# Eight dense chunks an image in every group, six indirect transfers under way, and shorter planned times for them

## The chip, the cores and the metric

The program runs on one core of a Trainium2 chip. The metric is the device time of one execution in microseconds. Five engines work side by side, each through its own queue in order: TensorE (PE in the profile, its weight loads PEld), VectorE (DVE), ScalarE (ACT), GpSimd (POOL) and SyncE (SP). Here SP issues the plain DMAs, and POOL issues only indirect ones (scatters and gathers of rows by a list of row numbers).

## The reference

The input is 32 images of 128 channels by 56 x 56 pixels, f32. Cut to what matters:

```python
x = x + conv3x3(sign(group_norm(x)), sign(w)) * Alpha      # 128 -> 128 channels
t = to_tokens(x)                                            # 3136 tokens of 128 numbers an image
n = layer_norm(t)
t = t + (n @ Wq) * sum_over_tokens((n @ Wk) * (n @ Wv))
n = layer_norm(t)
p = softmax(n @ router_w); top_p, top_i = top_k(p, 2)       # 8 experts, two of them a token
top_p = top_p / sum(top_p)
t = t + sum_k top_p[k] * (n @ expert_w[top_i[k]])           # and expert_b
out = from_tokens(t)
```

So every token goes through two of eight 128 x 128 expert matrices, and its result is put back where it came from.

## The kernel before

An image's 3136 tokens are cut into 25 chunks of 128 (the last has 64); four chunks make a block. The first stages (convolution, statistics, the token product, the projection, the router) run for every image alike. The experts are done in one of two ways.

**Dense.** The first `DENSE[group]` chunks of an image take all eight experts and weight them by gates that are zero for the six not chosen. For a block, `spread` (line 1087, its broadcast 1096, on SP) loads the gates of two experts at a time, broadcast over 128 partitions (`bc`, 512 KB); `gated` (1105, DVE) multiplies the tokens by them; `experts` (1117 and 1123, PE) sums the products in one bank; `finish` (1134, DVE) adds; `store` (1139) writes out. A block is four such units of two experts, after one turn of its tokens to channels (1078 PE, 1085 ACT).

**Sorted.** The remaining chunks of an image are sorted by pair of experts. `pair_of`, `places` and `row_numbers` (lines 1200 to 1280) give each token a row in a list of its group; `row_add` (1319, ACT) finishes a chunk's rows, and `scatter` (1325, POOL) writes its 128 rows to the list in DRAM with one indirect DMA. When all images of a group are scattered, its tiles are worked through in quads of four: `tile_load` (1617, SP), `tile_turn` (1624, PE), `tile_turned` (1630, ACT), `tile_experts` (1642, PE: just the two experts of the tile), `tile_read` (1660 and 1667, ACT), `tile_sum` and `tile_out` (1672, 1677, DVE), `tile_store` (1685, SP). When all tiles of a group are stored, `gather` (1400, POOL) brings the results of each chunk back with one indirect DMA; `back_turn` (1415, PE), `back_out` (1423, ACT) and `back_store` (1427, SP) write a block of four chunks out.

The 28 first images form groups of 8, 8, 8 and 4. The last four images belong to no group and are wholly dense, so that they lie beside the last group's tiles and gathers. Three places tie POOL to the other engines: an image's token buffer (three of them, tile `tok`) is free for the next image only when all its scatters have landed; a group's first tile load waits for all its scatters; a group's first gather waits for all its tile stores, and each gather needs one of 14 buffers that `back_turn` empties.

**What sets the order.** Nothing is issued in the order of the loops. Each step is entered with `at(due, key, engine, work, ...)`: a due time, an engine, a planned duration, the steps it follows, the rings of buffers that it takes and frees, and `delay`, the planned time until its result has landed. `in_order` (line 108) plays these steps through on a clock of its own, always taking, of the steps that can start first, the most urgent one, and so writes down one order for all engines. PE, DVE and ACT then run in exactly that order; POOL's and SP's instructions stand in it too. The durations there are constants in the source and not times of the chip; a wrong one changes only the order. A POOL step, scatter or gather, is planned at 2.0, a gather lands 12.0 after it, and in the plan POOL takes one step at a time.

`in_turn` (line 1475) adds a real wait: each indirect transfer waits until the one `IN_FLIGHT` places before it has landed, so that at most four are under way.

Of the kernel before, what the change touches and what calls it, by code (L numbers as in the profile page):

```python
# [66 lines left out]
ROW = C + 4  # L67
N_PAIR = N_EXP * (N_EXP - 1) // 2
GROUPS = (8, 8, 8, 4)
DENSE = (8, 8, 12, 12)  # L70

IN_ORDER = {mybir.EngineType.PE, mybir.EngineType.DVE, mybir.EngineType.Activation}
NEWTON = 3
IN_FLIGHT = 4

GATE_LANDS, SPREAD_LANDS, STORE_LANDS, TILE_LANDS, GATHER_LANDS = 5.0, 6.5, 5.0, 6.0, 12.0
TILE_PACE = (0.7, 0.6, 0.4, 0.3)
GATHER_PACE = (1.0, 0.8, 0.5, 0.4)
N_Q = C + 2 * N_EXP
# [98 lines left out]
def conv_attn_moe_kernel(  # L178
# [35 lines left out]

    most = n_ck - min(DENSE)
    group_of, last_of = {}, []
    for g, n in enumerate(GROUPS):
        for _ in range(n):
            group_of[len(group_of)] = g
        last_of.append(len(group_of) - 1)  # L220
    group_rows = [n * (n_tok - k * C) for n, k in zip(GROUPS, DENSE)]
    region = max(group_rows) + C
# [230 lines left out]
    def at(due, key, engine, work, do, *args, after=(), take=(), free=(), delay=0.0, slack=0.0):  # L453


        if isinstance(work, float):
            steps[key] = Step(due, key, engine, work, do, args, after, take, free, delay, slack, 0.0)
            return
        running = []

        def go_on():
            if not running:
                running.append(do(*args))
            next(running[0], None)

        lag = LAG if isinstance(work, list) else 0.0
        for j, w in enumerate(work):
            last = j == len(work) - 1
            part = key if last else (*key, "part", j)
            steps[part] = Step(  # L470
                due, part, engine, w, go_on, (), [(*key, "part", j - 1)] if j else after,
                [] if j else take, free if last else [], delay if last else 0.0, slack, lag,
            )

    def base(i):

        n = len(group_of)
        return P * (min(i, n) + 1.2 * max(0, i - n))
# [39 lines left out]
    def last_dense(i):  # L518
        return DENSE[group_of[i]] // PER - 1 if i in group_of else n_blk - 1

    def plan_image(i: int):
        s = base(i)
        d = {}
        st1, st2, lgp = st1_all[i % 2], st2_all[i % 2], lgp_all[i % 2]
        move = move_all[i % 2]
        n_dense = DENSE[group_of[i]] if i in group_of else n_ck
        n_sort = n_ck - n_dense
# [135 lines left out]
        for g in range(n_blk):  # L663
            b = min(n_conv - 1, (cols_of(g)[1] - 1) // (ROWS * width))
            due = s + 4 + 5.5 * b
# [689 lines left out]
        for k, c in enumerate(range(n_dense, n_ck)):  # L1355
            at(
                s + 138 + 2 * k, ("row_add", i, c), "ACT", 0.30, row_add, c,
                after=[("row_scalars", i), ("row_numbers", i), ("project_add", i, c // Q_GROUP)],
                take=["sent"],
            )  # L1360
            at(
                s + 140 + 2 * k, ("scatter", i, c), "POOL", 2.0, scatter, c,
                after=[("row_add", i, c), ("row_numbers", i), ("open", group)],
                free=[("tok", ("xt", i, 0)), ("sent", ("row_add", i, c))], delay=3.0,
            )
# [65 lines left out]
        begin, each = gather_due(group)  # L1431
        due = begin + each * (i - last_of[group] + GROUPS[group] - 1)
# [5 lines left out]
        k = 0  # L1438
        for b in range(n_dense // PER, n_blk):
            share = len(blocks[b]) / PER  # L1440
            for c in blocks[b]:
                at(
                    due + each * k / n_sort, ("gather", i, c), "POOL", 2.0, gather, c,
                    after=[("result_rows", i)]
                    + [("gather", i, c - 1) if k else ("gather", i - 1, n_ck - 1)]
                    + [("tile_store", group, q) for q in range(quads_of(group))],
                    take=["back"], delay=GATHER_LANDS,
                )
                k += 1
            at(  # L1450
                due + each * k / n_sort + 5, ("back_turn", i, b), "PE", 0.45 * share, back_turn, b,
                after=[("gather", i, c) for c in blocks[b]], take=["ps"],
                free=[("back", ("gather", i, c)) for c in blocks[b]],
            )
            at(
                due + each * k / n_sort + 6, ("back_out", i, b), "ACT", 0.47 * share, back_out, b,
                after=[("back_turn", i, b)], take=["o"], free=[("ps", ("back_turn", i, b))],
            )
            at(
                due + each * k / n_sort + 8, ("back_store", i, b), "SP", 0.35, back_store, b,  # L1460
                after=[("back_out", i, b)], free=[("o", ("back_out", i, b))], delay=STORE_LANDS,
            )
# [12 lines left out]
    def in_turn(dma):  # L1475

        before = moved[-IN_FLIGHT:][:1] if len(moved) >= IN_FLIGHT else []
        for b in before:
# [10 lines left out]
    def quads_of(g):  # L1489
        return -(-tiles_of(g) // PER)  # L1490
# [5 lines left out]
    def gather_due(g):  # L1496

        begin, each = tiles_due(g)
        return begin + each * quads_of(g) + 15, GATHER_PACE[g] * P
# [187 lines left out]
    def plan_group(g):  # L1687
# [29 lines left out]
        for q in range(quads_of(g)):  # L1717
# [4 lines left out]
                + [("tile_load", g, q - 1) if q else ("tile_load", g - 1, quads_of(g - 1) - 1)]  # L1722
                + [("scatter", i, c) for i in members for c in range(DENSE[g], n_ck)],
                take=["t_in"], delay=TILE_LANDS,
# [37 lines left out]
    for i in range(n_img):  # L1762
        plan_image(i)
# [57 lines left out]
```

## Time and profile before

| what | value |
|---|---|
| median of 14 runs | 2242.15 us (2235.4 to 2251.95) |
| profiled execution, its own time | 2251.51 us |
| span from first to last instruction | 2249.7 us |
| PE busy | 2093.0 us, 93% of the span |
| DVE busy | 1977.2 us, 88% |
| ACT busy | 1526.3 us, 68% |
| POOL busy | 1009.5 us, 45%, nearly all in 428 scatters and 428 gathers |
| granted TensorE clock, mean | 0.973 |
| DMA moved | 448.56 MB |

The profile is of one execution, which took 9.4 us more than the median. Busy time is the time in which an engine had at least one instruction under way. A row of the groups gives line, engine, operation, tiles written and read, shapes and count, then busy time and the mean duration of one instruction (they overlap on PE, so that count times mean is more than busy), then the idle time just before them and what ended it. An f32 matrix product stands as two instructions. The chain is followed back from the last instruction, at each step to whatever released it; its shares say in which work the end was waited for.

### The profile page before, as it was taken

Reading aid. Unit: us, or ns where it says so; the run is one execution under the profiler, and the core shown is the slowest. Engines: PE = TensorE matmul, PEld = TensorE weight load, DVE = VectorE, ACT = ScalarE, POOL = GpSimd, SP = SyncE. Lnnn points to the kernel's source line nnn. Section 1 sums busy time; section 2 is a strip of 40 time slices with the busy share of each in tenths; the row PEclk is TensorE's granted clock in tenths of the full one; section 3 lists DMA queues with packets and bytes.
Section 4 is the critical chain, followed back from the end, with each engine's and each line's share of the span. In section 5 each row is a group of like instructions: output and inputs, shape, how many; then the busy total and the mean of one; then the engine's idle time right before and its main releaser. Section 6 shows DMA issues by size and latency. Waiting matters only on the chain.

```text
span 2249.7 us, 45155 instructions
## 1 busy us (share of the span) xinstructions
PE 2093.0 (93%) x12074; PEld 1445.0 (64%) x12074; DVE 1977.2 (88%) x6360; ACT 1526.3 (68%) x4883; POOL 1009.5 (45%) x971
## 2 busy tenths in 40 slices
PE   4889998999999999989998999999699989999989
PEld 2656665566777777656776777666477765676644
DVE  3799999999999999999897999999688968779875
ACT  3766667667888897658987887656488966573411
POOL 1033444442232224554555554655555555424564
PEclk9989999999999999999999999999899999999999
DMA  4034454546565655567777766667577766877797
GB/s 171 30 133 138 160 166 155 172 133 205 169 186 175 189 185 181 170 192 243 220 225 223 233 199 208 217 213 231 184 219 232 252 197 213 262 221 249 242 303 278
DMA packets 317740, 448.56 MB, mean 199 GB/s; under 512 B 61065, under 2 KB 223153, under 8 KB 317490
## 3 DMA queue, kind: packets, MB, share of 16 engines
q1 hardware_dynamic: 289090, 386.97, 54.5%
q0 software_dynamic: 27392, 55.17, 7.9%
q10 hardware_dynamic: 1008, 3.54, 0.4%
q8 instruction: 102, 1.67, 0.3%
q14 instruction: 148, 1.21, 0.2%
HBM read 319.51 MB, written 126.00 MB: 198 GB/s over the span
## 4 chain that ended last, share of the span: by engine, by line
PE 61%; DVE 24%; DMA 7%; issue 3%; ACT 3%; SPq 2%; POOL 0%; DVEq 0%; ACTq 0%; POOLq 0%
PE ff L1123 21%; PE cv L601 11%; PE to L1642 9%; PE gram L703 6%; PE q L822 5%; DVE gated L1105 4%; DVE tok L774 3%; DVE st L641 3%; PE turn L1624 2%; DVE x L612 2%; DVE st L856 2%; DMA bc<-gp 2%; PE xt L628 2%; PE back_ps L1415 1%; DMA t_in<-rows 1%
## 5 line engine op out<-in xcount | busy, mean ns | idle before, releaser
L1325 POOL DMA_INDIRECT rows<-tok,row_no x428 | 504.8, 1179 | 740.3 <-ACT tok L1319 349.4
L1123 PE MATMUL ff<-gated,ew_d 128*128 128x512 f32 (+1 forms) x1536 | 723.3, 601 | 36.3 <-DVE gated L1105 35.8
L1400 POOL DMA_INDIRECT back<-res,res_no x428 | 495.3, 1157 | 483.3 <-PE back_ps L1415 140.6
L1105 DVE TENSOR_TENSOR gated<-tt,bc 128x1024 f32<-128x1024 f32 x384 | 450.3, 1178 | 99.8 <-PE ff L1123 55.6
L1123 PEld LDWEIGHTS ff<-gated,ew_d 128*128 128x128 f32 x1536 | 279.0, 196 | 277.2 <-issue 204.2
L601 PE MATMUL cv<-xs,w_bin 128*128 128x448 bf16 x2016 | 422.7, 358 | 6.1 <-ACT xs L567 4.1
L1660 ACT ACTIVATE v<-to,t_in 128x128 f32<-128x128 f32 x528 | 251.9, 477 | 91.7 <-PE to L1642 88.4
L601 PEld LDWEIGHTS <-w_bin 128*128 128x128 bf16 x2016 | 197.4, 99 | 181.0 <-issue 26.8
L1642 PEld LDWEIGHTS to<-ew_s,turned 128*128 128x128 f32 x2112 | 257.3, 193 | 39.1 <-issue 20.2
L836 ACT ACTIVATE qs<-q,r 128x136 f32<-128x136 f32 (+1 forms) x800 | 244.5, 402 | 53.2 <-PE q L822 39.9
L694 ACT ACTIVATE y<-tok,r 128x128 f32<-128x128 f32 (+1 forms) x800 | 252.5, 406 | 39.5 <-DVE r L512 26.5
L1642 PE MATMUL to<-ew_s,turned 128*128 x2112 | 269.7, 277 | 9.5 <-ACT tok L634 4.7
L822 PE MATMUL q<-move,x 128*128 128x144 f32 (+1 forms) x1600 | 238.1, 296 | 7.0 <-ACT qs L840 4.9
L822 PEld LDWEIGHTS q<-move,x 128*128 128x128 f32 (+1 forms) x1600 | 213.3, 193 | 35.1 <-issue 9.9
L703 PEld LDWEIGHTS gram<-y 128*128 128x128 f32 (+1 forms) x1600 | 199.5, 191 | 34.0 <-issue 21.1
L703 PE MATMUL gram<-y 128*128 128x129 f32 (+1 forms) x1600 | 211.3, 278 | 0.0
L1667 ACT ACTIVATE w<-to,t_in 128x128 f32<-128x128 f32 x528 | 204.9, 388 | 0.0
L641 DVE BATCH_NORM_STATS2 st<-tok 128x6 f32<-128x128 f32 (+1 forms) x800 | 178.8, 276 | 20.4 <-ACT tok L634 20.1
L856 DVE BATCH_NORM_STATS2 st<-tok 128x6 f32<-128x128 f32 (+1 forms) x800 | 194.6, 281 | 0.0
L612 DVE SCALAR_TENSOR_TENSOR x<-cv,alpha_col,x 128x448 f32<-128x448 f32 x224 | 151.2, 675 | 33.2 <-PE cv L601 32.9
L634 ACT COPY tok<-xt 128x512 f32<-128x512 f32 (+1 forms) x224 | 116.5, 563 | 88.9 <-PE xt L628 60.1
L1319 ACT ACTIVATE tok<-tok,a 128x128 f32<-128x128 f32 (+1 forms) x428 | 172.4, 433 | 0.1
(216 smaller groups left out, 2867.8 us busy)
## 6 DMA issues: line engine op xcount, KB each, us to landing
bc<-gp SPq DMA_DIRECT2D x368, 512.0 KB
x<-in_x_dram SPq DMA_DIRECT2D x64, 784.0 KB
t_in<-rows SPq DMA_DIRECT2D x528, 66.0 KB
res<-v SPq DMA_DIRECT2D x132, 256.0 KB
out_dram<-o SPq DMA_DIRECT2D x100, 256.0 KB
out_dram<-tt SPq DMA_DIRECT2D x92, 256.0 KB
rows<-zeros SPq DMA_DIRECT2D x116, 66.0 KB
rows<-tok,row_no POOLq DMA_INDIRECT x428
```

What stands on the lines that cost most here:

```text
L601: nc.tensor.matmul(cv, lhsT=w_bin[:, t, :], rhs=xs[:, b * ROWS + dy : b * ROWS + dy + ROWS, dx : dx + width], start=(t == 0), stop=(t == T ...
L641: nc.vector.bn_stats(st[:n, c, :], d["tok"][:n, c, :C])
L694: nc.scalar.mul(y[:n, j, :C], d["tok"][:n, c, :C], d["r1"][:n, c : c + 1])
L703: nc.tensor.matmul(d["gram"], lhsT=y[:n, j, :C], rhs=y[:n, j, :], start=(c == 0), stop=(c == n_ck - 1),)
L822: nc.tensor.matmul(p[:n, k, :], lhsT=d["x"][:, c * C : c * C + n], rhs=move, start=True, stop=True,)
L836: nc.scalar.mul(qs[:n, k, : C + N_EXP], p[:n, k, : C + N_EXP], d["r1"][:n, c : c + 1])
L1105: nc.vector.tensor_tensor(g[:, :, :n], d["tt", b][:, :n].unsqueeze(1).to_broadcast([C, 2, n]), d.pop(("bc", b, k))[:, :, :n], ALU.mult,)
L1123: nc.tensor.matmul(d["ff", b][:, :n], lhsT=ew_d[:, e * C : (e + 1) * C], rhs=g[:, j, :n], start=False, stop=(e == N_EXP - 1),)
L1325: dma = nc.gpsimd.indirect_dma_start(out=groups[group]["rows"], out_offset=bass.IndirectOffsetOnAxis(ap=d["row_no"][:n, c - n_dense : c - ...
L1400: dma = nc.gpsimd.indirect_dma_start(out=d["back", c][:n, :], out_offset=None, in_=groups[group]["res"][: quads_of(group) * WIDE, :], in_o ...
L1642: nc.tensor.matmul(p[:, k, j, :], lhsT=t[:, n * C : (n + 1) * C], rhs=ew_s[:, bass.ds(d["cols", q][j][n], C)], start=True, stop=True,)
L1660: nc.scalar.activation(d["v", q][:, n, :], p[:, k, 0, :], AF.Identity, bias=row[:, C + 2 : C + 3], scale=row[:, C : C + 1],)
```

## The change

Three constants of the plan and one count change. Groups 2 and 3 (images 16 to 27) had twelve dense chunks an image and thirteen sorted ones; now all groups have eight dense and seventeen sorted ones. Six indirect transfers may be under way at a time instead of four. In the plan a gather lands after 9.0 instead of 12.0, and a scatter or gather occupies POOL for 1.5 instead of 2.0.

```diff
 GROUPS = (8, 8, 8, 4)
-DENSE = (8, 8, 12, 12)
+DENSE = (8, 8, 8, 8)
...
-IN_FLIGHT = 4
-
-GATE_LANDS, SPREAD_LANDS, STORE_LANDS, TILE_LANDS, GATHER_LANDS = 5.0, 6.5, 5.0, 6.0, 12.0
+IN_FLIGHT = 6
+
+GATE_LANDS, SPREAD_LANDS, STORE_LANDS, TILE_LANDS, GATHER_LANDS = 5.0, 6.5, 5.0, 6.0, 9.0
...
             at(
-                s + 140 + 2 * k, ("scatter", i, c), "POOL", 2.0, scatter, c,
+                s + 140 + 2 * k, ("scatter", i, c), "POOL", 1.5, scatter, c,
                 after=[("row_add", i, c), ("row_numbers", i), ("open", group)],
...
                 at(
-                    due + each * k / n_sort, ("gather", i, c), "POOL", 2.0, gather, c,
+                    due + each * k / n_sort, ("gather", i, c), "POOL", 1.5, gather, c,
                     after=[("result_rows", i)]
```

In the built program, one dense block leaves each of twelve images: 96 of 736 full expert products (1123), 48 of 368 full `gated` multiplications (1105), 48 full broadcasts `bc`, 36 loads of `gt`, 12 `finish` and 12 `store`. Added are 48 scatters and 48 gathers (428 of each become 476), 12 quads of tiles (132 become 144: 8 in group 2, 4 in group 3), 48 turns of the way back (1415) with 12 `back_out` and `back_store`, 48 `row_add`, and a little more of the sorting arithmetic on DVE and PE for those images. The order differs on every engine from image 2 on, since the plan's times enter everywhere.

## The prediction

> **What bounds the kernel now.** First the page: busy shares and the shares of the chain that ended last, for all and by line.
>
> ```profile
> PE 2093.0 (93%) x12074; PEld 1445.0 (64%) x12074; DVE 1977.2 (88%) x6360; ACT 1526.3 (68%) x4883; POOL 1009.5 (45%) x971
> ...
> PE 61%; DVE 24%; DMA 7%; issue 3%; ACT 3%; SPq 2%; POOL 0%; DVEq 0%; ACTq 0%; POOLq 0%
> ```
>
> ```profile
> by line: PE ff L1123 20.7%; PE cv L601 10.7%; PE to L1642 9.3%; PE gram L703 6.1%; PE q L822 4.9%; DVE gated L1105 4.1%; issue 2.9%; DVE tok L774 2.6%; DVE st L641 2.5%; PE turn L1624 2.3%; DVE x L612 1.9%; DVE st L856 1.8%; DMA bc<-gp 1.8%
> ```
>
> PE carries the end for 61% and DVE for 24%; the largest item is the dense expert product, a fifth of the span. POOL, at 45%, is as good as never on the chain. Second, stretches of time (busy us and counts for PE, PEld, DVE, ACT, POOL, then clock, DMA share, GB/s):
>
> ```profile
> 900.00:1550.00 650.00, 625.16 (x3696) 435.78 (x3695) 599.08 (x1976) 471.84 (x1514) 355.77 (x302) 0.98 0.69 216
> 1550.00:1600.00 50.00, 35.37 (x178) 23.14 (x177) 30.38 (x95) 20.69 (x69) 28.72 (x24) 0.86 0.39 122
> 1600.00:1800.00 200.00, 194.33 (x1251) 145.88 (x1252) 178.79 (x564) 166.05 (x528) 104.68 (x91) 0.98 0.77 241
> 1800.00:1900.00 100.00, 87.34 (x477) 59.83 (x476) 74.05 (x218) 57.78 (x177) 56.68 (x49) 0.93 0.68 203
> 1900.00:2050.00 150.00, 146.55 (x869) 106.35 (x868) 116.17 (x275) 99.04 (x301) 65.91 (x60) 0.99 0.79 241
> 2050.00:2250.00 200.00, 180.61 (x683) 100.82 (x681) 153.17 (x336) 47.94 (x141) 102.48 (x86) 0.95 0.81 270
> ```
>
> PE is busy 96 to 98% in most and 90% in the tail, but idles 14.6 us in 1550 to 1600 and 12.7 us in 1800 to 1900: there groups 2 and 3 have their last scatters out and their tiles not yet in. POOL issues only 302 transfers in the 650 us from 900 on, one in 2.15 us. Third, the waits:
>
> ```profile
> POOL back L1400 <- PE back_ps L1415: 140.6, 43, 17.8
> ...
> POOL back L1400 <- DMA rows<-tok,row_no: 89.9, 30, 6.5
> ...
> POOL back L1400 <- DMA back<-res,res_no: 39.3, 48, 3.9
> ```
>
> POOL waits 140.6 us for PE to empty gather buffers, and 129.2 us for an earlier transfer to land, which is mostly the limit of four. Its own speed is a different number, from the rows of the two tiles (ns least, median, most):
>
> ```profile
> L1325 POOL DMA_INDIRECT rows<-tok,row_no x428: 898/992/3417, 123.8 to 1884.9; - x143
> ...
> L1400 POOL DMA_INDIRECT back<-res,res_no x428: 904/972/3559, 883.3 to 2232.8; - x143
> ```
>
> Their means are 1179 and 1157 ns (page), and 0.30 us lies between two that follow without a wait (timeline): 1.17 + 0.30 = 1.47 us a transfer.
>
> **The change part by part.** Eight dense chunks for twelve images. Busy us and mean ns by shape:
>
> ```profile
> L1123 PE MATMUL ff<-gated,ew_d 128*128 128x512 f32 x1472 | 714.0, 615 | 35.2 <-DVE gated L1105 34.6
> ...
> L1105 DVE TENSOR_TENSOR gated<-tt,bc 128x1024 f32<-128x1024 f32 x368 | 445.6, 1216 | 88.8 <-PE ff L1123 46.7 <-DMA bc<-gp 35.3 <-PE back_ps L1415 4.2
> ...
> L1642 PE MATMUL to<-ew_s,turned 128*128 x2112 | 269.7, 277 | 9.5 <-ACT tok L634 4.7 <-ACT turned L1630 2.1 <-ACT move L765 0.6
> ```
>
> PE, an image: 16 instructions of L1123 at 714.0/1472 = 0.485 us are 7.76; the bias product L1117 36.1/92 = 0.39; the turn L1078 55.8/92 = 0.61; one of two gate turns (L981) 0.21. Removed: 8.97. Added: a quad, L1642 269.7/132 = 2.04 and L1624 83.8/132 = 0.63; the way back L1415 61.1/100 = 0.61; four more columns of `places` 0.8, from its rows at 13 and 17 chunks. Added: 4.08. Net 4.9, and 59 us for twelve.
>
> DVE: removed 4 x 445.6/368 = 4.84, `finish` 0.68, smaller gate arithmetic 0.12; added `tile_sum` and `tile_out` 0.68 + 0.69, six sorting operations at 0.65 instead of 0.53 us (0.69), `hot_sum` 0.14. Net 3.4, or 41 us. ACT grows: removed L1085 0.60; added L1423 0.60, `row_add` 4 x 161.1/400 = 1.61, and a quad's 0.61 + 1.91 + 1.55 = 4.07. Net 5.7, or 68 us. Of that about 45 (eight quads, and the extra `row_add` and ways back) fall in 1600 to 1900, where ACT has 300 - 223.8 = 76 us idle: I cost it at nothing; if that cover were gone it is at worst the 68. POOL: 96 x 1.47 = 141 us, hidden in the 1000 us and more that it idles; with no cover it would lengthen the end as the POOL rival does. SP: 96 issues go (48 `bc`, 36 `gt`, 12 `gb`) and 48 tile loads with 12 result stores come, and 12 `out` stores change lines: fewer in all, and no step is moved past another queue by hand. 25 MB of broadcasts leave, 13 MB of rows come; nothing charged.
>
> Not all PE time is end time, so the sum goes by the chain. Of 92.5 full dense blocks 12 go, 13.0%; of 132 quads 12 come, 9.1%; of 107 ways back 12, 11%. On 2249.7 us: ff 20.7% = 465.7, so -60.5; gated 4.1% = 92, -12.0; bc 1.8% = 40, -5.3; to 9.3% = 209, +19.0; turn 2.3% = 52, +4.7; back_ps 1% = 22, +2.5. Sum -51.6. PE busy alone says -59; I take the chain, which counts only work that was waited for.
>
> What comes back: a token buffer is freed by an image's last scatter. The trace shows that wait (L634 on rows) once in 1550 to 1600, 15.8 us, and once in 1800 to 1900, 6.3. Four more scatters before it are 4 x 1.47 = 5.9 us, in two places 11.8. Bounds: zero if POOL catches up, and above the POOL rival.
>
> Six under way instead of four: at most the 129.2 us of POOL's waits go, but POOL is not on the chain, and the gather's next wait is the buffer that PE empties; I charge 0, with the idle PE of 27.3 us in the two stretches as the upper gain. Below zero it could be a loss if transfers that share the DMA engines land later: those take 2 to 7 us now, and the plan allows a gather 9; a PE wait for a gather appears once, 6.2 us (the waits of PE), so I bound it by that, for each of the two groups' starts, 12 us.
>
> The plan's 1.5 and 9.0: they only reorder. 1.5 is what the row says (1.47), the old 2.0 was too long; so the order stops holding POOL back, and PE steps behind gathers come earlier. In 150 to 500 DVE is busy 343.7 of 350 us: nothing there for an order to win. I charge 0.
>
> A rule that speaks against this: the Trainium skill, SBUF — State Buffer, section Who interferes with whom, says that a VectorE instruction with two SBUF inputs, as `gated` is, holds up a GpSimd instruction that reads SBUF, and that one of the two blocks fully. By it each added transfer could stand behind one `gated`, 1.2 us, making 96 x 1.2 = 115 us more of POOL. The trace has the mean only 0.19 us above the median, with single ones of 3.5; no run here shows the cause.
>
> Sum: -51.6 + 11.8 = -39.8. The profiled execution, 2251.51 us, would become 2212; its median lies 9.4 lower, so against 2242.15 it is **2202**.
>
> **The rivals.** (1) POOL becomes the end: slower. From 1885 on POOL only gathers, 78 in 1885 to 2085 and 76 in the last 150 us:
>
> ```profile
> 2085.00:2235.00 150.00, 90.53 (x76) 0.94 0.86 284
> ```
>
> That is 1.97 us each, of which the wait for buffers is 30.7 us; without it 1.57. With 32 + 16 more, about 202 gathers follow the last scatter, which comes some 50 us earlier (1835), and 17 us follow the last gather: 1835 + 202p + 17. At 1.57 it ends at 2169, hidden; it equals today's 2250 at p = 1.97. At 2.1 the span is 2276 and the median frame 2268. For it: 1.97 is just what the tail shows, and the DMA share there is 0.86. Against: that pace is the plan's own 2.0. At p = 1.9 the median is 2228.
>
> (2) Nothing comes back and the two stalls go too: -51.6 - 27.3 = -78.9, 2163. For it: clock and PE fall exactly where scatters end. Against: more scatters, not fewer, precede these tiles.
>
> (3) ACT becomes the bound: it takes 46.6 of 50 us in 1750 to 1800 already. All 68 us on the path against PE's 59 gives +9, 2251; it decides once the added 45 us exceed the 76 idle.
>
> (4) The change does not do what it says: blocks leave where DVE or DMA set the pace, gain gone elsewhere, 2225 to 2242. Against: ff has 20.7% of the chain.
>
> **How the numbers follow.** Forecast 2202 (2185 to 2220) 0.59; rival 2 0.17; rival 1 0.12, of which 0.07 at paces above 1.97; rival 3 0.05, 0.03 of it slower; rival 4 0.07, half of it within 0.2%. About 0.2%, 4.5 us, is the least that a measurement of this kernel tells from no change. Slower: 0.07 + 0.03 = 0.10; same 0.04; faster 0.86. For 8 in 10 the range goes from 2166, just above rival 2, to 2240, which takes in rival 1 up to 1.9 us and rival 4.
>
> **What the profile after would show.** L1123 at 1280 full instructions, about 620 us; L1105 near 388; PE busy near 2034, DVE 1936, ACT 1594; POOL with 952 transfers and the wait for landed ones well under 129. Right if PE keeps at least 93% of a shorter span. Wrong if POOL paces the tail above 1.97 us a gather, if PE waits for gathers appear (many lines of back_ps on DMA), or if idle PE grows beyond today's 157 us by more than 12.

## The result, and the profile after

| | before | after |
|---|---|---|
| median | 2242.41 us (47 runs) | 2270.2 us (10 runs, 2265.42 to 2276.7) |
| profiled span | 2249.7 us | 2263.2 us |
| PE busy / idle in the span | 2093.0 / 157 us | 2053.9 / 209 us |
| granted TensorE clock, mean | 0.973 | 0.961 |

The ratio is 1.012, with a 95% interval of 1.0102 to 1.0139. The kernel became slower; the forecast was 2202 us with a range to 2240. PE did lose work, 39 us of busy time, but its idle time grew by 53. That makes 13.4 us, as the two profiled executions differ (2264.9 against 2251.51 us); the other 14 of the medians' 28 us lie in no profile, since the one of before took 9 us more than its median and the one of after 5 less.

First the page's line of busy times, of after:

```profile
PE 2053.9 (91%) x12148; PEld 1445.2 (64%) x12148; DVE 1946.2 (86%) x6336; ACT 1571.4 (69%) x5039; POOL 1100.7 (49%) x1067
```

PE's share fell from 93 to 91% although it has less to do. The chain of after can't tell where it stands: its shares add up to 27% of the span, against 100 before. The stretches of time do (busy us and counts for PE, PEld, DVE, ACT, POOL, then clock, DMA share, GB/s):

```profile
150.00:500.00 350.00, 326.82 (x1815) 212.75 (x1814) 341.75 (x1246) 230.74 (x774) 132.40 (x115) 0.97 0.46 147
500.00:900.00 400.00, 394.09 (x2538) 289.40 (x2537) 385.56 (x1282) 341.82 (x1110) 132.13 (x120) 1.00 0.60 185
900.00:1550.00 650.00, 589.49 (x3595) 419.19 (x3594) 573.11 (x1970) 478.52 (x1545) 393.59 (x342) 0.96 0.62 193
1550.00:1600.00 50.00, 35.12 (x205) 26.58 (x204) 35.75 (x133) 27.38 (x90) 33.30 (x29) 0.86 0.53 171
1600.00:1800.00 200.00, 176.94 (x1170) 136.75 (x1169) 158.61 (x489) 159.06 (x505) 119.88 (x110) 0.94 0.65 197
1800.00:1900.00 100.00, 89.41 (x569) 68.18 (x568) 74.69 (x232) 78.15 (x248) 23.24 (x19) 0.95 0.61 181
```

Up to 900 us PE's idle time is what it was: 23.2 and 5.9 us. From 900 to 1550 it is 60.5 us (24.8 before), and from 1600 to 1800 it is 23.1 (5.7 before): 53 us more, which is all of the growth. There the scatters of later groups and the gathers of earlier ones (the first at 886 us) run side by side. POOL, which had 302 transfers in the 650 us, now has 342.

How PE stands still is seen best where nothing else runs either. The three longest stops of after, from the last instruction before a stop to the first after it (same columns):

```profile
1490.50:1507.50 17.00, 0.00 (x0) 0.00 (x0) 0.00 (x0) 0.00 (x0) 8.61 (x9) 0.50 0.41 113
1565.00:1573.90 8.90, 0.00 (x0) 0.00 (x0) 0.00 (x0) 0.00 (x0) 5.38 (x6) 0.72 0.16 46
1637.90:1650.20 12.30, 0.00 (x0) 0.00 (x0) 0.00 (x0) 0.00 (x0) 6.39 (x8) 0.61 0.26 88
```

For 38.2 us PE, DVE and ACT have not a single instruction under way, and of the computing engines POOL alone works through its queue. Before had such stops too; its two longest come to 16.6 us:

```profile
1581.20:1594.00 12.80, 0.00 (x0) 0.00 (x0) 0.00 (x0) 0.00 (x0) 6.91 (x8) 0.62 0.13 39
1812.70:1816.50 3.80, 0.00 (x0) 0.00 (x0) 0.00 (x0) 0.00 (x0) 1.75 (x2) 0.99 0.78 243
```

With those of 2 us and more it is 48 us after and 22 before. So 26 of the 53 us of idle time that PE gained are stops of the whole core; in the rest another engine still works.

What POOL does in the longest stop is in the timeline of after (start, us, instruction, idle before it and what ended that):

```profile
1489.05 0.96 POOL L1325 DMA_INDIRECT rows<-tok,row_no  x1 [0.30 <-issue]
...
1491.46 0.92 POOL L1400 DMA_INDIRECT back<-res,res_no  x1 [1.45 <-issue]
1496.95 0.98 POOL L1400 DMA_INDIRECT back<-res,res_no  x1 [4.56 <-DMA rows<-tok,row_no]
...
1505.12 0.92 POOL L1325 DMA_INDIRECT rows<-tok,row_no  x1 [0.30 <-issue]
1506.35 0.95 POOL L1400 DMA_INDIRECT back<-res,res_no  x1 [0.30 <-issue]
1507.61 0.58 ACT L634 COPY tok<-xt 128x512 f32<-128x512 f32 x1 [22.22 <-DMA rows<-tok,row_no]
```

Gathers (L1400) and scatters (L1325) take turns in one queue. ACT's copy of a new image into its token buffer (L634) waits 22.22 us, until the scatters of the image that had the buffer have landed; and those stand behind a gather that itself waits 4.56 us. PE and DVE work in their written order behind that copy. In the waits of after that wait is a line of its own (us in all, places, longest); it was 22.7 us in 3 places before. The second line is DVE's wait for the same copy; it was 20.1 us in 15 places:

```profile
ACT tok L634 <- DMA rows<-tok,row_no: 87.7, 10, 22.2
DVE st L641 <- ACT tok L634: 83.9, 23, 19.5
```

Image by image the traces show it too. Until the gathers begin, an image's last scatter is issued at most 4 us after its row is finished; for the images 14 to 26 it comes 7 to 31 us after it, in both kernels. In after the copy that takes the buffer again starts 1.3 to 2.5 us after the end of that scatter for every image from 14 to 25; before, only the images from 22 on were as close (1.4 to 3.7 us), the eight ahead of them had 6 to 46 us to spare.

So the picture of after is this: scatters come late out of POOL's queue, a token buffer comes free late, and the whole core stops for it. Theory A, as the expectations call it, says that POOL's lateness is the cause. It leaves open whether the number of transfers or the place of the scatters makes it late. The rivals lay the loss on the new constants: the shorter planned times, or six transfers that get in each other's way.

### The profile page after: what moved, and what is told of

Its sections match the earlier page's. It is cut to its first block, busy times and chain, and to the rows that moved or that the text cites. A ratio compares the mean times of both kernels' runs of the same rounds, so it can differ in the third digit from the quotient of the medians.

```text
span 2263.2 us, 45671 instructions
## 1 busy us (share of the span) xinstructions
PE 2053.9 (91%) x12148; PEld 1445.2 (64%) x12148; DVE 1946.2 (86%) x6336; ACT 1571.4 (69%) x5039; POOL 1100.7 (49%) x1067
## 5 line engine op out<-in xcount | busy, mean ns | idle before, releaser
L1325 POOL DMA_INDIRECT rows<-tok,row_no x476 | 558.2, 1173 | 737.6 <-ACT tok L1319 401.6
L1400 POOL DMA_INDIRECT back<-res,res_no x476 | 533.1, 1120 | 416.9 <-issue 91.6
L1123 PE MATMUL ff<-gated,ew_d 128*128 128x512 f32 (+1 forms) x1344 | 627.3, 596 | 28.0 <-DVE gated L1105 27.7
L1105 DVE TENSOR_TENSOR gated<-tt,bc 128x1024 f32<-128x1024 f32 (+1 forms) x336 | 392.7, 1173 | 92.0 <-PE ff L1123 52.5
L1123 PEld LDWEIGHTS ff<-gated,ew_d 128*128 128x128 f32 x1344 | 243.2, 195 | 235.9 <-issue 179.5
L1660 ACT ACTIVATE v<-to,t_in 128x128 f32<-128x128 f32 x576 | 276.0, 480 | 79.8 <-PE to L1642 78.5
L1642 PEld LDWEIGHTS to<-ew_s,turned 128*128 128x128 f32 x2304 | 281.9, 193 | 54.7 <-issue 19.1
L1642 PE MATMUL to<-ew_s,turned 128*128 x2304 | 295.1, 278 | 21.4 <-ACT tok L634 14.0
L641 DVE BATCH_NORM_STATS2 st<-tok 128x6 f32<-128x128 f32 (+1 forms) x800 | 183.8, 276 | 84.4 <-ACT tok L634 83.9
L634 ACT COPY tok<-xt 128x512 f32<-128x512 f32 (+1 forms) x224 | 121.0, 567 | 157.4 <-DMA rows<-tok,row_no 87.7
L1667 ACT ACTIVATE w<-to,t_in 128x128 f32<-128x128 f32 x576 | 225.2, 391 | 0.0
L1423 ACT COPY o<-back_ps 128x512 f32<-128x512 f32 (+1 forms) x140 | 73.7, 531 | 141.2 <-PE back_ps L1415 86.4
```

The source lines that it names most:

```text
L1105: nc.vector.tensor_tensor(g[:, :, :n], d["tt", b][:, :n].unsqueeze(1).to_broadcast([C, 2, n]), d.pop(("bc", b, k))[:, :, :n], ALU.mult,)
L1123: nc.tensor.matmul(d["ff", b][:, :n], lhsT=ew_d[:, e * C : (e + 1) * C], rhs=g[:, j, :n], start=False, stop=(e == N_EXP - 1),)
L1325: dma = nc.gpsimd.indirect_dma_start(out=groups[group]["rows"], out_offset=bass.IndirectOffsetOnAxis(ap=d["row_no"][:n, c - n_dense : c - ...
L1400: dma = nc.gpsimd.indirect_dma_start(out=d["back", c][:n, :], out_offset=None, in_=groups[group]["res"][: quads_of(group) * WIDE, :], in_o ...
L1642: nc.tensor.matmul(p[:, k, j, :], lhsT=t[:, n * C : (n + 1) * C], rhs=ew_s[:, bass.ds(d["cols", q][j][n], C)], start=True, stop=True,)
L1660: nc.scalar.activation(d["v", q][:, n, :], p[:, k, 0, :], AF.Identity, bias=row[:, C + 2 : C + 3], scale=row[:, C : C + 1],)
```

## The experiments

All are edits of the kernel before or of the changed one, and each ratio is against runs of the kernel before on the same chip. On some of the chips the kernel before took 2242 to 2255 us, on others 2312 to 2324; so the two kinds are kept apart, and across them nothing but ratios is compared. A changed due time changes more than the steps that bear it: `in_order` writes the order of all engines anew.

### The parts of the change one at a time

**Eight chunks alone.** In the kernel before:

```diff
-DENSE = (8, 8, 12, 12)
+DENSE = (8, 8, 8, 8)
```

> Only the dense chunks change (8, 8, 8, 8); four under way, planned times 2.0 and 12.0 as before. Theory A (the order asks for a transfer every 1.5 us where POOL does one in 1.84, 185 in the 340 us from 1380 on, so scatters land late and token buffers come free late): the order is honest about POOL, but it now spaces 952 transfers at 2.0, so POOL paces the end: 2270 to 2340. Theory B (sorted chunks cost more than dense ones, whatever the order): about 2265, as with the whole change. Theory C (six under way make every transfer land later): the gain of 40 us that was predicted appears, about 2200.

2324.68 us against 2249.3, ratio 1.0345 (1.031 to 1.0379). The chunks alone cost 75 us; everything else in the change wins some of that back. The stretch of the stops, of this run:

```profile
900.00:1550.00 650.00, 591.55 (x3543) 417.56 (x3542) 574.21 (x1936) 463.85 (x1502) 353.41 (x315) 0.96 0.62 192
```

PE's idle time there is 58.5 us, as in the changed kernel, but POOL has got 27 transfers less done in it. Waits of L634 for other things than its input, and DVE's for it:

```profile
ACT tok L634 <- issue: 18.9, 3, 10.2
ACT tok L634 <- DMA back<-res,res_no: 11.4, 1, 11.4
DVE st L641 <- ACT tok L634: 43.7, 21, 10.9
```

Only 8.3 us of L634's are put down to scatters, but the names mislead here. The three longest stops of the whole core (8.3, 4.3 and 7.5 us) end with this very copy at 1162, 1305 and 1379 us, each 3.6 to 5.2 us after the start of the last scatter that the buffer waited for. So late token buffers hold this kernel up too. Its stops are short, though, beside the 78 us of idle time that PE has gained in all; where the rest comes from stays open.

**Six under way alone, twice.**

```diff
-IN_FLIGHT = 4
+IN_FLIGHT = 6
```

> Only the limit of transfers under way changes, 4 to 6; the order is that of the kernel before, instruction for instruction. A and B: 2242 within 10, since POOL's waits for landed transfers (129 us) were not on the path. C: 2260 or more.

> The kernel before with six transfers under way and nothing else, again, on whatever chip comes here. Where the kernel before takes 2242 to 2249 us: 0.992 to 0.997 as the first time. Where it takes 2310 us and more: the whole change and the change with four under way stood there within 0.2% of each other, so I expect six under way to be worth nothing there, 0.995 to 1.005; the rival, that six under way is worth its 0.6% on every chip, expects 0.992 to 0.997 there too.

2240.3 against 2249.3, 0.9944 (0.9918 to 0.997), and 2240.99 against 2255.06, 0.9932 (0.9907 to 0.9957). Six under way is worth about 0.6% without the chunks. In the traces PE, DVE and ACT run in the order of the kernel before, instruction for instruction; POOL does not, 228 of its 971 instructions stand up to seven places elsewhere, so the 0.6% is for both. A transfer lands 2 to 7 us after its issue, as with four: its last DMA packet ends 3.7 us after the start (median) with four, 3.8 with six. The rival of transfers that get in each other's way falls. The second run came to a chip of the 2250 us kind, so the other half of its expectation was not tried.

**The plan's two constants alone.**

```diff
-... GATHER_LANDS = 5.0, 6.5, 5.0, 6.0, 12.0
+... GATHER_LANDS = 5.0, 6.5, 5.0, 6.0, 9.0
-s + 140 + 2 * k, ("scatter", i, c), "POOL", 2.0, scatter, c,
+s + 140 + 2 * k, ("scatter", i, c), "POOL", 1.5, scatter, c,
-due + each * k / n_sort, ("gather", i, c), "POOL", 2.0, gather, c,
+due + each * k / n_sort, ("gather", i, c), "POOL", 1.5, gather, c,
```

> Only the planned times change (1.5 and 9.0); 856 transfers, four under way. A: the same fault on fewer transfers: the wait of ACT L634 for landed scatters rises above its 22.7 us, but POOL is less full; 2225 to 2255. B: a better order without the cost of the chunks, 2200 to 2235. C: 2242 within 10.

2248.76 against 2249.3, 1.0003 (0.9985 to 1.0022): nothing, as forecast for this part alone. With the old chunks it does no harm on this chip. Parts do not add up here: +3.45, -0.6 and 0.0% make +2.8, and the whole measures +1.2.

### Is it POOL's transfers?

**Half of the gathers left out of the changed kernel.**

```diff
+if (c - n_dense) % 2:
+    d["back", c] = d["back", c - 1]
+    return
```

> The changed kernel in its own order, but every second gather of an image is left out (its tile is the neighbour's, so half of the sorted outputs are wrong): POOL has 224 to 232 transfers fewer, all else stands. A: scatters no longer queue behind gathers, ACT L634 waits for landed scatters 30 us or less instead of 88, and the time falls by the idle PE of the middle, to 2190 to 2215. B: only the gathers' own share goes, 2245 to 2265. C: in between.

2201.0 against 2249.3, 0.9779 (0.9759 to 0.98). Half of the sorted outputs are then wrong. The order of PE, DVE and ACT is the changed kernel's, instruction for instruction in the traces; only every second gather is gone from POOL's queue, and the ratio goes from 1.012 to 0.978, some 77 us. The row of 900 to 1550, the wait of L634 and DVE's for it:

```profile
900.00:1550.00 650.00, 611.63 (x3792) 441.16 (x3790) 600.55 (x2090) 500.16 (x1617) 329.58 (x278) 0.97 0.62 190
```

```profile
ACT tok L634 <- DMA rows<-tok,row_no: 15.3, 4, 11.2
DVE st L641 <- ACT tok L634: 26.3, 18, 9.0
```

PE is 22 us busier in the stretch, and the waits fall from 87.7 to 15.3 us and from 83.9 to 26.3. With every other step in its place, this shows that half of the gathers cost the changed kernel these 77 us. It leaves out 224 transfers, more than the 96 that the change adds, so it does not price those. And two things went with the gathers' places in POOL's queue: 15 of 435 MB of DMA traffic, and half of their use of the 14 buffers; neither was tried apart.

**Half of the gathers left out of the kernel before, twice** (the same edit):

> The kernel before with every second gather left out (the neighbour's tile stands in for it, so half of the sorted outputs are wrong); its order unchanged. If POOL is off the path there, as the chain of waits says (POOL 0%): 2235 to 2250. If late transfers hold it back too: 2200 to 2225, with the idle PE of 1550 to 1600 and 1800 to 1900 (27 us) gone.

> The kernel before with every second gather left out (the neighbour's tile stands in for it, so half of the sorted outputs are wrong), once more, beside a kernel before that is not disturbed. If POOL is off the path there, as the chain of waits says (POOL 0%): 2235 to 2250. If late transfers hold the kernel before back too: 2200 to 2230.

2228.51 against 2318.31, 0.9629 (0.9593 to 0.9665), and 2226.53 against 2312.14, 0.9645 (0.9589 to 0.9701). So the kernel before was held back by its gathers too, on chips of the slower kind by 3.6%, although its chain on such a chip gives POOL 0% as well.

### The number of transfers, or the place of the scatters?

**Scatters earlier in the changed kernel's order, twice.**

```diff
-s + 140 + 2 * k, ("scatter", i, c), "POOL", 1.5, scatter, c,
+s + 90 + 2 * k, ("scatter", i, c), "POOL", 1.5, scatter, c,
```

> The changed kernel, with the due time of every scatter 50 earlier, so that of several transfers that POOL could issue the plan takes scatters before gathers; nothing else. If scatters are late because gathers stand before them in POOL's queue (A1): ACT L634 waits for landed scatters under 45 us, and 2205 to 2240. If POOL simply has more transfers than it can do there, whatever their order (A2): gathers are late instead and PE waits for those, 2255 to 2285.

> The changed kernel with every scatter's due time 50 earlier, once more. If scatters are late because gathers stand before them in POOL's queue (A1): ratio 0.98 to 0.998. If POOL has more transfers than it can do in the middle, whatever their order (A2): the wait of ACT L634 for scatters shrinks, other waits grow, ratio 1.005 to 1.02.

2369.24 against 2318.31, 1.0206 (1.0167 to 1.0244), and 2371.52 against 2312.14, 1.0268 (1.0203 to 1.0332). Beside 1.012 this looked like a loss, and I took it for the number of transfers. It was the wrong yardstick, as the next run showed.

**The changed kernel itself on a chip of the slower kind,** with the kernel before for its profile:

> The changed kernel, unchanged, beside the kernel before on this chip. On an ordinary chip: the ratio 1.012 again, 1.009 to 1.015. On a chip where the kernel before takes 2300 us: theory A expects the ratio to stay above 1.01, since more transfers meet a later POOL, 1.01 to 1.04; theory C expects 1.012 there too.

> The kernel before, unchanged, run for its own profile on whatever chip comes here. If the chip gives it its 2242 to 2249 us, the profile is the one already known (900 to 1550: PE near 625 us, POOL near 302 transfers) and nothing is learnt. If the chip gives it 2300 us and more, theory A (POOL late in its in-order queue) expects the loss of 60 to 70 us in 900 to 1900, POOL's full stretch of 340 us near 2.3 us a transfer or above, and 150 to 500 and 500 to 900 within 4 us of PE's 327 and 394; theory C (that chip is slower everywhere) expects every stretch to lose about 3%.

The changed kernel: 2407.5 against 2323.76, 1.0392 (1.0328 to 1.0456). So on such chips the change costs 3.9%, and scatters first win back a third to a half of it (1.0206 and 1.0268, on other chips of that kind). The kernel before: 2314.29, 0.9979 (0.9943 to 1.0016). Its windows, on this chip:

```profile
150.00:500.00 350.00, 327.29 (x1820) 213.20 (x1819) 343.83 (x1259) 232.51 (x782) 137.46 (x119) 0.98 0.45 149
500.00:900.00 400.00, 388.27 (x2474) 287.04 (x2473) 375.49 (x1229) 338.15 (x1092) 125.82 (x113) 0.99 0.59 183
```

That chip is not slower everywhere: 150 to 500 is the same (327.29 against 326.67), and most of the loss lies after 900, where POOL's two kinds of transfers meet. But 500 to 900 already loses 6 us, more than the 4 that was expected, POOL's mean instruction is no longer (1137 and 1145 ns, against 1179 and 1157), and its pace in 1380 to 1720 is 2.21 us (154 transfers) against 2.17, not 2.3. Many waits in that chip's profiles have no releaser on record. What differs between the chips stays open.

**Scatters earlier and six under way, without the added transfers.** In the kernel before:

```diff
-IN_FLIGHT = 4
+IN_FLIGHT = 6
-s + 140 + 2 * k, ("scatter", i, c), "POOL", 2.0, scatter, c,
+s + 90 + 2 * k, ("scatter", i, c), "POOL", 2.0, scatter, c,
```

> The kernel before with six under way and with its scatters due 50 earlier in the order. Where it is the late scatters that hold the token buffers (theory A), scatters first helps also without the added transfers: on a chip where the kernel before takes 2310 us and more 0.975 to 0.995, since there the changed kernel with scatters first stood 1.2 to 1.8% under the changed kernel; on an ordinary chip, where the kernel before waits for the scatters 22.7 us in all, 0.985 to 0.996. If it is the number of transfers alone, it stands where the flight-only kernel beside it stands, within 0.3%, or above it, since gathers are put later.

2205.52 us (2202.88 to 2214.86) against 2255.06, ratio 0.9799 (0.9771 to 0.9827): faster than both kernels, and than the 0.985 that was expected at best. Against the flight-only kernel on the same chip it is 35 us, 1.6%, from one constant and no transfer fewer. The two rows where the kernel before had its stalls, first of the flight-only kernel, then of this one:

```profile
1550.00:1600.00 50.00, 40.22 (x185) 24.48 (x184) 39.96 (x134) 25.98 (x82) 28.97 (x24) 0.90 0.62 198
1800.00:1900.00 100.00, 88.73 (x503) 62.45 (x503) 75.29 (x209) 61.79 (x189) 56.16 (x52) 0.97 0.73 216
```

```profile
1550.00:1600.00 50.00, 50.00 (x320) 38.35 (x320) 45.00 (x136) 44.24 (x139) 28.85 (x26) 1.00 0.83 247
1800.00:1900.00 100.00, 95.94 (x563) 68.13 (x562) 84.83 (x239) 68.24 (x212) 62.70 (x53) 1.00 0.82 253
```

PE is full in the first and has 4.1 us idle in the second, the clock is 1.00, and POOL issues as many transfers as before (26 and 53, against 24 and 52). POOL's total is unchanged: 856 transfers, 1013.7 us busy (997.2 in the flight-only kernel). So their number alone did not cost these stalls. DVE's wait for L634, first of the flight-only kernel, then of this one:

```profile
DVE st L641 <- ACT tok L634: 25.1, 16, 6.4
DVE st L641 <- ACT tok L634: 10.5, 15, 2.2
```

Where the buffers come free the traces show directly: in the flight-only kernel the last scatter of each of the images 22 to 27 ends 1.3 to 5.2 us before the copy that takes its buffer again, in this one 16 to 50 us before it. But the one constant did more than move scatters. 160 of the 428 have fewer gathers before them, 20 at the most, and from 941 us on the orders of PE, DVE and ACT are others too (5196 of 12074 PE instructions stand elsewhere). In 1550 to 1600 the flight-only kernel's long wait is DVE's for a broadcast `bc`, 9.5 us, and not for a scatter. So it is shown that the buffers came free earlier and were waited for less; how much of the 35 us that gave, and how much the rest of the new order, is not. For the changed kernel both number and place seem to count: half the gathers out gave 3.4%, and the same constant won back a third to a half of the loss on the slower kind of chip. It was not run on a chip of the other kind.

### Whether the two aids can be told apart

**The change with four under way, with 1.75 planned, and the aids without the chunks.** The edits are `IN_FLIGHT = 4`, and 1.75 for 1.5 in both lines, in the changed kernel; `DENSE = (8, 8, 12, 12)` in it, three times; and `IN_FLIGHT = 6` with 1.75 and 12.0 in the kernel before.

> The whole change with four under way instead of six: dense 8, 8, 8, 8 and the shorter planned times. Theory A: the two aids of the change act together; without the two more places POOL waits for landings again, so slower than the change itself, 1.02 to 1.035 of the kernel before on an ordinary chip, with POOL near 1.9 us a transfer or above in 1380 to 1720. If it is within 0.3% of the changed kernel, six under way adds nothing, and the shorter planned times alone win back what lies between 1.0345 and 1.012.

> The changed kernel with 1.75 instead of 1.5 planned for a transfer. If the harm is an order that is tighter than POOL (1.84 us a transfer): the wait of ACT L634 falls to 30 to 60 us, and 2240 to 2270. If POOL's number of transfers bounds the middle and the order can only add to that: between the whole change and the dense chunks alone (ratio 1.034 at 2.0), 2275 to 2305.

> The changed kernel with the dense chunks of before (8, 8, 12, 12): six under way, 1.5 and 9.0. 856 transfers. If the chunks carry all the loss, this is the sum of the two other parts, 0.994 x 1.000: 2225 to 2245. If planned times that are too short harm by themselves, as soon as the transfers are not limited to four: 2255 or more.

> Six under way, 1.5 and 9.0, dense chunks as before (8, 8, 12, 12), once more. If the chunks carry all the loss of the change, this is the product of the two parts measured alone, 0.994 x 1.000: 2225 to 2240, ratio 0.990 to 0.998. If planned times that are too short do harm when four no longer limit POOL: ratio 1.005 or more.

> Six under way and the plan's shorter times, with the old 8, 8, 12, 12 dense chunks. Theory A, on an ordinary chip: each of the two did little alone (0.9944 and 1.0003), and without the added transfers POOL is not pressed, so together 0.985 to 1.002. The rival, that the shorter planned times let POOL fall behind whatever the number of transfers, expects above 1.005, as on the slower chips (1.010 and 1.015).

> The kernel before with six under way and 1.75 planned for a transfer (gathers still landing after 12.0, dense chunks as before). An order that fits POOL's own pace of 1.84 better than 2.0 does, for 856 transfers: 2215 to 2240, ratio 0.985 to 0.998; if the order is worth nothing: 0.994, as six under way alone.

All of these fell on chips of the slower kind:

| kernel | us | before there | ratio, interval |
|---|---|---|---|
| change, four under way | 2416.72 | 2323.76 | 1.0406 (1.0346 to 1.0466) |
| the change itself | 2407.5 | 2323.76 | 1.0392 (1.0328 to 1.0456) |
| change, 1.75 planned | 2396.01 | 2318.31 | 1.0348 (1.031 to 1.0387) |
| aids without chunks | 2345.44 | 2318.31 | 1.0099 (1.0061 to 1.0137) |
| the same | 2348.49 | 2312.14 | 1.0146 (1.0079 to 1.0213) |
| the same | 2363.09 | 2323.76 | 1.0185 (1.0133 to 1.0238) |
| flight and 1.75 without chunks | 2324.99 | 2312.14 | 1.0066 (1.0032 to 1.01) |

On these chips six under way adds nothing to the change. The aids without chunks lose 1 to 1.9% there, and 1.75 in place of 1.5 (with 12.0 for 9.0) loses less, though 0.2 to 1.5% were expected to be won. That fits an order that counts on a faster POOL than there is, but neither aid was run alone there, so it is not shown. On the other kind of chip each aid alone cost nothing, and which of them wins back 50 of the chunks' 75 us there stays open. A fourth token buffer, which would give the scatters more time, was not tried.

## Why the prediction was wrong

**The step that failed** is what comes back: "Four more scatters before it are 4 x 1.47 = 5.9 us, in two places 11.8". The mechanism was right: a token buffer freed by late scatters. Its size and its places were not. The wait grew from 22.7 to 87.7 us, at 10 places, and PE's idle time by 53 us where the sum had 11.8. Between the forecast of the profiled execution, 2212, and its 2264.9 us lie 53: 41 of them are this term, the other 12 that PE's busy time fell by 39 us and not by the chain's 51.6. Two assumptions made the term small.

- *POOL's pace.* 1.47 us is the pace between transfers that wait for nothing. Where scatters and gathers share the queue the pace is another, here POOL's row and its two groups in 1380 to 1720 of after (busy, mean ns, then idle and what ended it):

```profile
1380.00:1720.00 340.00, 207.01 (x185) 0.91 0.55 174
```

```profile
L1400 POOL DMA_INDIRECT back<-res,res_no x105 | 115.1, 1096 | 95.6 <-issue 32.5 <-DMA rows<-tok,row_no 23.6 <-PE gram L703 16.0
L1325 POOL DMA_INDIRECT rows<-tok,row_no x80 | 92.3, 1154 | 37.6 <-issue 16.8 <-ACT qs L840 5.6 <-ACT tok L1319 4.4
```

340/185 is 1.84 us each; the prediction's own row of 900 to 1550 had one in 2.15. Alone this makes 7.4 us out of the 5.9, so it is the smaller part. The scatters themselves wait little, 37.6 us for 80; the 105 gathers wait 95.6, and every scatter behind a waiting gather waits along.

- *What a late scatter stands behind.* I counted the four scatters that are new, and not the gathers of the groups before that lie between the scatters in the same queue; 48 more of those came too. Nor is it only the new scatters: the first of the ten waits stands behind image 15, which has seventeen sorted chunks in both kernels, so there only the order and the limit have changed. What each gave to the 65 us was not told apart.

**"POOL: 96 x 1.47 = 141 us, hidden in the 1000 us and more that it idles"** failed with it. Instructions of POOL cost 91 us more, 0.95 each and 1.25 with the 0.30 between two, so that term was even too high; but idle time of an in-order queue that lies in waits hides nothing from what is queued behind. And **"POOL, at 45%, is as good as never on the chain"** was read as "does not bound". With half its gathers gone the kernel before runs 3.6% faster on one kind of chip, and with six under way and its scatters due earlier 2.0% faster on the other: a late scatter appears on the chain as a wait for a DMA, if at all, and the written order has the other engines' work spaced around it.

**The PE and DVE terms** were of the right kind. L1123 with 512 columns has 1280 instructions and 617.9 us, L1105 388.1 (about 620 and 388 forecast). PE busy was to fall 59 us and fell 39. With half the gathers out the same PE work took 2041.9 us at a mean clock of 0.974, not 2053.9 at 0.961: 12 of the 20 are gone there, in a run that has 11 us of stops of the whole core where the changed kernel has 48; in a long stop and just behind it the clock is granted at half (last section). DVE fell 31 of 41, ACT rose 45 of 68, and ACT is not the bound (rival 3).

**Six under way**, charged 0 with 27.3 as the upper gain, gave 13 and 15 us alone, inside the bounds. **The plan**, charged 0, gave 0 alone on the first kind of chip. "1.5 is what the row says (1.47), the old 2.0 was too long; so the order stops holding POOL back" is half true: with six under way it wins back 50 us of what the chunks cost there; but the order then counts on 1.5 in a stretch where the pace is 1.84, and that POOL falls behind it fits the ten waits and is not shown apart from the chunks.

**The rivals.** POOL as the end was the right rival in the wrong place. I put it in the tail, to decide at 1.97 us a gather. The tail of after, in the same window as before's 76 gathers:

```profile
2085.00:2235.00 150.00, 111.58 (x97) 0.94 0.88 290
```

97 gathers, 1.55 us each. The 1.97 was how the old order spaced them (with six under way it has 74 in that window), and the tail is not where it was lost. Rival 2, that the two stalls go, did not come: PE's idle time is 14.9 and 10.6 us in them (14.6 and 12.7 before), and new stops came beside them. With scatters due earlier they all but go. The rule that was weighed (the Trainium skill, SBUF — State Buffer, Who interferes with whom) would have made the indirect instructions slower, if it bears on them; their means are 1173 and 1120 ns after, 1179 and 1157 before, so that is not what was lost. The named sign of failure, idle PE beyond 157 by more than 12, is what came: 209.

## What to carry to other kernels

Ask of an in-order queue not how busy it is but what stands in it behind something that waits, and who needs that; price an added instruction there by the pace in the stretch where the kinds mix and by all that stands before it, not by the gap between two that wait for nothing. Where transfers that free a scarce buffer share a queue with transfers that wait for one, try to put the former first: here the constant that did so was worth 1.6%, with all that it changed in the other engines' order. An idle share of the chain is no proof that an engine does not bind when the order of all others was written around it.

## What the runs showed of the hardware that I had not expected

- A long stop costs more than its length. In after the granted clock is 0.50 over the stop at 1490 us and still half in the first 5 us behind it, with PE at work again:

```profile
1507.50:1512.50 5.00, 4.25 (x18) 3.37 (x19) 4.27 (x18) 3.78 (x8) 3.58 (x4) 0.50 0.45 134
```

- The kernel with scatters first, with PE busy throughout 1550 to 1600, has a clock of 1.00 there, and its PE busy time is 12.4 us shorter than the flight-only kernel's (2076.0 against 2088.4) for the same instructions in another order.
- Two kinds of chips: the kernel before takes 2242 to 2255 us on one, 2312 to 2324 on the other; 150 to 500 us are alike, and with half the gathers gone it takes 2226 to 2229 on the second. The price of the same change is 1.2% on the one and 3.9% on the other.
- Six indirect transfers under way land as soon as four, 2 to 7 us after the issue (median 3.8 and 3.7).
